# Four edits around the end of the attention stage and the quantized feed-forward: norms in halves, an early gelu table, clamping on ScalarE, and a bias added later

## The chip, the core and the metric

The kernel runs on one core of a Trainium2 chip. A core has engines that run their own instruction streams side by side and meet only at semaphores: TensorE (PE, matrix products; its weight loads are shown as PEld), VectorE (DVE, elementwise work and reductions), ScalarE (ACT, activation functions and copies), GpSimd (POOL, elementwise work) and SyncE (SP, which only issues transfers here). Each engine issues its own stream in order. PE writes its products into a small memory of its own, PSUM; everything else lies in the on-chip memory SBUF. The metric is the device time of one execution in microseconds. Before the change it is 938.37 us, the median of five runs from 937.44 to 939.41.

## What is computed

The input `x` is 32 sequences of 128 tokens of 128 numbers, and so is a context. The reference adds four layers to `x`, each behind a layer norm and a tanh gate:

```python
x = x + jnp.tanh(g_xattn[0]) * _L0_xattn_ref(_layernorm(x, axis=-1), ctx_1024, ctx_1024, ...)
x = x + jnp.tanh(g_ffn[0]) * _L0_ffn_ref(_layernorm(x, axis=-1), ...)
x = x + jnp.tanh(g_xattn[1]) * _L1_xattn_ref(ctx_1024, _layernorm(x, axis=-1))
x = x + jnp.tanh(g_ffn[1]) * _L1_ffn_ref(_layernorm(x, axis=-1), ...)
```

The first layer is an attention of eight heads whose scores are multiplied by decays (an exponential of gates), with a norm of each head's output. The second is a feed-forward with both inputs quantized to 8 bits over the whole tensor:

```python
scale = jnp.maximum((amax - amin) / 255.0, 1e-08)
zp = jnp.clip(jnp.round(-amin / scale) + QMIN, QMIN, QMAX)
q = jnp.clip(jnp.round(x / scale) + zp, QMIN, QMAX)
```

so no token can be quantized before the least and the greatest number of all 32 normed sequences are known; then product with W1, exact gelu, the same quantization again over all hidden values, product with W2, and `+ b`. The third layer aligns the sequences by dynamic time warping, the fourth is a mixture of eight experts with a global threshold. The change touches the end of the first layer and the second.

## The kernel before

Tokens lie on the 128 partitions, one sequence beside the other: `X` is [128, 32, 128]. `YT` holds the normed `X` transposed. A scheduler orders each engine's instructions from the traced program: the earlier traced goes first among those that it takes to be ready, and what is ready may pass what waits. `tc.issue_after(i)` around an instruction puts it behind `i` on the same engine, with no other wait. Tile pools give each tag a fixed number of buffers (`bufs`).

**The attention loop** runs over n = 0 to 32. Round n makes the scores of sequence n+1 on PE (`scores`, L469), and for each half hf of the heads `values(n, hf)`: DVE multiplies scores by decays (`sm`, L505), PE multiplies with the values (L507); then `decays(n+1, hf)`: two products into `bi` (L484, L485) and ACT's exponential `dm` (L490). Every second round ACT copies the product (`ats`, L514), PE transposes it (L523), ACT copies and squares (L527, L529) and DVE takes the denominators (`mxd`, `d2`, L531 to L538): `outputs`.

Every eight sequences a generator `finish(q, ...)` does what is left for them, in steps that the loop takes two at a time behind each half (`for _ in range(2): next(behind, None)`): ACT squares `d2` (L543); DVE makes `qv` (L545) and a reciprocal root in ten small instructions on 64 columns (`root_steps`, L167 to L174), multiplies the heads by it and by the gain and adds to `X` (L557, L562, L567, twice each on 512 columns); then `norm_steps`: bn_stats for each sequence (L140), five small instructions (L145 to L153) and a second root on 8 columns, then for each sequence `y` (L189, four buffers) and its transpose on PE (L192), and for each four sequences `take`: ACT copies into `YT` (L446), DVE reduces greatest and least (`xst`, L448, L449). Sequences 0 to 7, 8 to 15 and 16 to 23 are done so while the next eight are in the loop; the last eight, 24 to 31, all after it.

**The feed-forward's scale.** DVE reduces `xst` (L620); `max_everywhere` (L205 to L213) spreads the two numbers over the partitions by two small PE products; `affine_scale` (L219 to L231) makes the scale, its reciprocal `inv`, the zero point and the bounds `lo` and `hi` in one-column DVE instructions. In the same place DVE makes `b2g` = gate x b2 (L628), and POOL adds it to all of `X` in four instructions (L630).

**The first product.** For each of four groups n of eight sequences and each half k, ACT scales and rounds 512 columns of `YT` (Identity with a large bias, L656), DVE clamps them (L657) and subtracts the bias into the 8-bit integers held as bf16, `XQ` (L659). For each of four chunks c PE multiplies (L664), ACT takes gelu (L669, 1024 columns) and DVE reduces greatest and least into `hst` (L673, L674). ACT also flips and squares context rows (`context_part`, L647 to L651) for the third layer. Then `hs2`, `max_everywhere` and `affine_scale` follow for the hidden values, and `dense` quantizes them with ACT's Relu and one DVE instruction (L708 to L712), the second product (L717) and the addition to `X` (L722).

Of the kernel before, what the change touches and what calls it, by code (L numbers as in the profile page):

```python
# [8 lines left out]
F32 = mybir.dt.float32  # L9
# [9 lines left out]
P = 128  # L19
# [19 lines left out]
def tile_flamingo_gated(  # L39
# [95 lines left out]

    def row_norm_steps(p, v, n, mean, r):

        bn = new(p, [P, n, 6], F32, "bn")
        for i in range(n):
            nc.vector.bn_stats(bn[:, i, :], v[:, i, :])  # L140
            if i % 2 == 1:
                yield

        df = new(p, [P, n], F32, "bn_df")
        nc.vector.tensor_tensor(df, bn[:, :, 1], bn[:, :, 4], ALU.subtract)  # L145
        ve = new(p, [P, n], F32, "bn_ve")
        nc.vector.scalar_tensor_tensor(
            ve, bn[:, :, 2], D * 1e-5, bn[:, :, 5], ALU.add, ALU.add
        )
        nc.vector.scalar_tensor_tensor(mean, df, -0.5, bn[:, :, 1], ALU.mult, ALU.add)  # L150
        yield
        nc.vector.scalar_tensor_tensor(df, df, 0.25, df, ALU.mult, ALU.mult)
        nc.vector.scalar_tensor_tensor(ve, ve, 1.0 / D, df, ALU.mult, ALU.add)  # L153
        yield
        for _ in root_steps(p, ve, n, r):
            yield

    def row_norms(p, v, n):
        mean = new(p, [P, n], F32, "bn_mean")
        r = new(p, [P, n], F32, "bn_r")  # L160
        for _ in row_norm_steps(p, v, n, mean, r):
            pass
        return mean, r

    def root_steps(p, v, n, r):

        nc.vector.tensor_scalar(  # L167
            r.bitcast(I32), v.bitcast(I32), -0.5, 1597463007.0, ALU.mult, ALU.add
        )
        t = new(p, [P, n], F32, "root_t")  # L170
        for _ in range(3):
            nc.vector.tensor_mul(t, r, r)
            nc.vector.scalar_tensor_tensor(t, v, -0.5, t, ALU.mult, ALU.mult)  # L173
            nc.vector.scalar_tensor_tensor(r, t, 1.5, r, ALU.add, ALU.mult)  # L174
            yield

    def norm_steps(p, psp, q, take, tag):

        xq = X[:, 8 * q : 8 * q + 8, :]
        mean = new(p, [P, 8], F32, "bn_mean")  # L180
        r = new(p, [P, 8], F32, "bn_r")
        for _ in row_norm_steps(p, xq, 8, mean, r):
            yield
        for h in range(2):
            tp = new(psp, [P, GB, S], F32, tag)
            for i in range(GB):
                j = GB * h + i
                y = new(p, [P, D], F32, "y", bufs=4)
                nc.vector.tensor_scalar(  # L189
                    y, xq[:, j, :], mean[:, j : j + 1], r[:, j : j + 1], ALU.subtract, ALU.mult  # L190
                )
                nc.tensor.transpose(tp[:, i, :], y, ident)  # L192
                if i % 2 == 1:
                    yield
            take(2 * q + h, tp)
            yield

    def norm_eight(p, psp, q, take, tag="tp"):
        for _ in norm_steps(p, psp, q, take, tag):
            pass  # L200
# [60 lines left out]
    with ExitStack() as st:  # L261
# [218 lines left out]
        def decays(n, hf):  # L480
            r, j, i = n // 16, n % 16 // 4, n % 4
            jr = slice(HW * j, HW * j + HW)
            bi = new(p_bi, [P, 4, S], F32, "bi")
            nc.tensor.matmul(bi, lhsT=identb, rhs=mneg, start=True, stop=False)  # L484
            nc.tensor.matmul(  # L485
                bi, lhsT=GP[jr, r, S * i : S * i + S], rhs=RH[r][jr, 4 * hf : 4 * hf + 4, i, :],
                start=False, stop=True,
            )
            dm = new(hp, [P, 4, S], F32, "dm", bufs=3)
            nc.scalar.activation(dm, bi, AF.Exp)  # L490
            held["dm", n, hf] = dm

        def values(n, hf):
# [11 lines left out]
            nc.vector.tensor_tensor(sm, held["sc", n][:, hf], held.pop(("dm", n, hf)), ALU.mult)  # L505
# [34 lines left out]
        def finish(q, HN, d2, ms):  # L540


            nc.scalar.activation(d2, d2, AF.Square, bias=small_c, scale=1e-3)  # L543
            qv = new(hp, [P, 64], F32, "qv")
# [5 lines left out]
            rr = new(hp, [P, 64], F32, "rr")  # L550
            for _ in root_steps(hp, qv, 64, rr):
                yield
            hf = HN.rearrange("p a x e -> p (a x) e")
            hg = HN.rearrange("p a (s h) e -> p (a s) (h e)", h=NH)
            for k in range(2):
                v = slice(32 * k, 32 * k + 32)
                nc.vector.tensor_tensor(  # L557
                    hf[:, v], hf[:, v], rr[:, v].unsqueeze(2).to_broadcast([P, 32, DH]), ALU.mult
                )
                yield  # L560
                v = slice(4 * k, 4 * k + 4)
                nc.vector.tensor_tensor(  # L562
                    hg[:, v], hg[:, v], gain.unsqueeze(1).to_broadcast([P, 4, D]), ALU.mult
                )
                yield
                xv = X[:, 8 * q + 4 * k : 8 * q + 4 * k + 4, :]
                nc.vector.tensor_tensor(xv, xv, hg[:, v], ALU.add)  # L567
                yield
            for _ in norm_steps(lp, p_at, q, take, "at"):
                yield  # L570
# [9 lines left out]
        for n in range(B + 1):  # L580
            if n < B:
# [6 lines left out]
                for hf in range(2):  # L588
# [5 lines left out]
                    for _ in range(2):  # L594
                        next(behind, None)
            else:
                outputs(n - 1, *tgt)
            if n % 8 == 0 and n:
                for _ in behind:
                    pass  # L600
                behind = finish(n // 8 - 1, *tgt)
# [14 lines left out]
    with ExitStack() as st:  # L616
        fp = pool(st, "ffn")
        HT = new(fp, [P, NC, B * S], F32, "HT")
        xs2 = new(fp, [P, 2], F32, "xs2")
        nc.vector.tensor_reduce(xs2, xst, AX.X, ALU.max)  # L620
        with ExitStack() as st2:
# [5 lines left out]
            b2g = new(fp, [P, D], F32, "b2g")  # L627
            nc.vector.tensor_scalar(b2g, b2s, tgf[:, 0:1], None, ALU.mult)  # L628
            for q in range(4):
                nc.gpsimd.tensor_add(  # L630
                    X[:, 8 * q : 8 * q + 8, :],
                    X[:, 8 * q : 8 * q + 8, :],
                    b2g.unsqueeze(1).to_broadcast([P, 8, D]),
                )
        hst = new(fp, [P, 2, 4 * NC], F32, "hst")
        with ExitStack() as st2:
# [16 lines left out]
            for n in range(4):  # L653
                for k in range(2):
                    blk = YT[:, 8 * n + 4 * k : 8 * n + 4 * k + 4, :].rearrange("p b s -> p (b s)")
                    nc.scalar.activation(blk, blk, AF.Identity, bias=magic_c, scale=inv)  # L656
                    nc.vector.tensor_scalar(blk, blk, lo, hi, ALU.max, ALU.min)  # L657
                    o = 1024 * n + 512 * k
                    nc.vector.tensor_scalar(XQ[:, o : o + 512], blk, MAGIC, None, ALU.subtract)  # L659
                for c in range(NC):  # L660
# [13 lines left out]
                    nc.vector.tensor_reduce(hst[:, 1, o : o + 1], hb, AX.X, ALU.min, negate=True)  # L674
                    if c % 2 == 1:
                        context_part(2 * n + c // 2)
        hs2 = new(fp, [P, 2], F32, "hs2")
# [15 lines left out]
        nc.vector.tensor_mul(s2, s2, tgf[:, 0:1])  # L693
        low = new(fp, [P, 2], F32, "low")
        nc.vector.tensor_scalar(low[:, 1:2], lo, -1.0, None, ALU.mult)
        tie = nc.vector.tensor_scalar(low[:, 0:1], lo, MAGIC, None, ALU.subtract)
# [56 lines left out]
        for n in range(NG):  # L753
# [3 lines left out]
            if n % 2 == 1:  # L757
                for _ in behind:
                    pass
                behind = norm_steps(lp, dps, n // 2, take, "tp")  # L760
# [325 lines left out]
```

## Time and profile before

| what | us |
|---|---|
| median of five runs | 938.37 |
| the profiled execution, and its span | 937.44, 935.7 |
| PE busy in the span | 689.4 (74%) |
| DVE busy | 579.4 (62%) |
| ACT busy | 370.5 (40%) |
| POOL busy | 28.5 (3%) |
| last reduction of the last norms ends | 212.01 |
| first gelu starts | 224.27 |
| last reduction of the gelu's results ends | 264.90 |

The stages follow each other in the span: attention until about 196 us, the last eight norms until 212, the scale of the tokens until 224, the first product until 265, the second product and the distances until 334, the warping until about 440, and the experts, more than half of the span, to the end. Times in the trace count from the span's start. A row of the timeline gives the start, the length, the engine, the line, the operation, the tile written and the tiles read with their shapes (partitions x elements), the number of instructions merged, and in brackets how long the engine had idled and for what. A row of stretches gives the bounds, the length and the busy time of each engine in it, then the granted PE clock (1 is full speed), the DMA's share and its GB/s.

### The profile page before, as it was taken

To read this page: it belongs to the slowest core of one execution; us is meant where nothing else is said; L and a number is where in the kernel's file an instruction comes from. 1 tells how busy PE (TensorE), PEld (TensorE's weight loads), DVE (VectorE), ACT (ScalarE), POOL (GpSimd) and SP (SyncE) were. 2 spreads that over 40 slices of the span, in tenths; PEclk is the share of its full clock that TensorE was granted. 3 is DMA by queue.
4 is the path that set the end of the run, shared out by engine and by line. 5 is a ranking of instruction groups with operands and counts; after the bars stand their busy time and mean duration, and the time that the engine had idled before them with its cause. 6 is when DMAs were issued, how large, how long until landed. Compare 5 with 4: busy or idle time off the path is not lost.

```text
span 935.7 us, 11340 instructions
## 1 busy us (share of the span) xinstructions
PE 689.4 (74%) x4026; PEld 445.1 (48%) x4026; DVE 579.4 (62%) x2011; ACT 370.5 (40%) x624; POOL 28.5 (3%) x66
## 2 busy tenths in 40 slices
PE   0769999933226700000799999999999999999998
PEld 0323333311025400000577767777777777777776
DVE  6665688989988769978666355799232223223232
ACT  1346666547635510000243444434334334334332
POOL 6000000003000000000000000000000000000000
PEclk9968899965556865555699999999999999999999
DMA  9000000031001244420000000000000000000000
GB/s 312 10 11 10 2 2 1 1 127 54 0 0 23 46 106 111 96 59 0 1 1 1 1 1 1 1 12 23 1 1 12 1 12 1 1 12 1 13 1 12
DMA packets 11409, 25.25 MB, mean 27 GB/s; under 512 B 2048, under 2 KB 6688, under 8 KB 10560
## 3 DMA queue, kind: packets, MB, share of 16 engines
q1 hardware_dynamic: 8872, 17.44, 6.2%
q10 hardware_dynamic: 2016, 6.30, 2.7%
q0 software_dynamic: 464, 0.79, 0.3%
q8 instruction: 31, 0.51, 0.2%
q14 instruction: 26, 0.21, 0.1%
HBM read 14.02 MB, written 4.46 MB: 20 GB/s over the span
## 4 chain that ended last, share of the span: by engine, by line
PE 59%; DVE 30%; ACT 4%; DMA 3%; issue 3%; ACTq 0%; DVEq 0%; POOLq 0%
PE mpo L1016 23%; PE mph L1007 20%; DVE ru L837 3%; DVE hit L883 2%; PE sc L469 2%; DVE hst L673 2%; DVE hst L674 2%; DVE ru L836 2%; DVE sm L505 2%; DMA CD<-in_ctx_d 2%; PE at L507 1%; DVE bn L140 1%; PE at L192 1%; PE d L731 1%; DVE root_t L173 1%
## 5 line engine op out<-in xcount | busy, mean ns | idle before, releaser
L1016 PEld LDWEIGHTS mpo<-mw2s,hT 128*128 128x128 f32 x2048 | 252.2, 192 | 62.6 <-issue 39.2
L1010 ACT ACTIVATE hT<-mph,mb1s 128x512 f32<-128x512 f32 x256 | 175.9, 687 | 238.0 <-PE mph L1007 236.3
L1016 PE MATMUL mpo<-mw2s,hT 128*128 128x128 f32 x2048 | 256.4, 276 | 0.1
L1007 PE MATMUL mph<-YT,mw1s 128*128 128x512 f32 x512 | 243.4, 598 | 0.0
L995 DVE SCALAR_TENSOR_TENSOR X<-mpo,GA,X 128x128 f32<-128x128 f32 x192 | 54.0, 343 | 198.1 <-PE mpo L1016 198.1
L1007 PEld LDWEIGHTS mph<-YT,mw1s 128*128 128x128 f32 x512 | 87.6, 192 | 61.9 <-issue 61.8
L995 DVE SCALAR_TENSOR_TENSOR X<-mb2s,GA,X 128x128 f32<-128x128 f32 x256 | 73.0, 342 | 0.0
L790 PE MATMUL gt_ps<-ident,ru 32*128 32x32 f32 x1 | 0.3, 282 | 77.5 <-DVE ru L837 77.5
L505 DVE TENSOR_TENSOR sm<-sc,dm 128x512 f32<-128x512 f32 x64 | 43.5, 684 | 21.8 <-ACT dm L490 18.3
L490 ACT ACTIVATE dm<-bi 128x512 f32<-128x512 f32 x64 | 37.9, 596 | 31.1 <-PE bi L485 28.5
L484 PE MATMUL bi<-mneg,identb 128*128 128x512 bf16 x64 | 26.4, 415 | 24.1 <-DVE identb L112 22.1
L469 PE MATMUL sc<-qm,CD 64*128 64x512 f32 x128 | 43.6, 693 | 0.0
L790 PEld LDWEIGHTS gt_ps<-ident,ru 32*128 32x128 f32 x1 | 0.2, 178 | 77.6 <-issue 77.6
L140 DVE BATCH_NORM_STATS2 bn<-X 128x6 f32<-128x128 f32 x128 | 33.2, 307 | 0.0
L873 ACT COPY dv<-vv 128x8 bf16<-128x8 bf16 (+1 forms) x5 | 1.1, 219 | 77.8 <-DMA rblk<-ru 48.0
L664 PE MATMUL ph<-XQ,w1q 128*128 128x512 bf16 x32 | 14.2, 533 | 23.6 <-DVE XQ L659 18.2
L192 PE MATMUL at<-ident,y 128*128 128x128 f32 x64 | 17.1, 383 | 18.7 <-DVE y L189 16.8
L507 PE MATMUL at<-sm,va 128*32 128x128 f32 x512 | 29.7, 297 | 1.0 <-DVE sm L505 0.8
L837 DVE TENSOR_TENSOR_SCAN ru<-ru,dc 64x128 f32<-64x128 f32 x64 | 26.6, 416 | 4.9 <-DMA dc<-d_dram 2.9
L189 DVE TENSOR_SCALAR y<-X,bn_mean,bn_r 128x128 f32<-128x128 f32 x96 | 27.2, 341 | 1.8 <-PE at L192 1.3
L485 PE MATMUL bi<-RH,GP 32*128 32x512 bf16 x64 | 26.0, 409 | 0.0
L507 PEld LDWEIGHTS at<-sm,va 128*32 128x32 f32 x512 | 11.3, 111 | 29.7 <-issue 7.3
(290 smaller groups left out, 811.2 us busy)
## 6 DMA issues: line engine op xcount, KB each, us to landing
X<-in_x SPq DMA_DIRECT2D x4, 512.0 KB, 11.8
CD<-in_ctx_d ACTq DMA_DIRECT2D x4, 512.0 KB, 10.7
CT<-in_ctx_t SPq DMA_DIRECT2D x4, 512.0 KB, 13.6
mw1s<-in_mw SPq DMA_DIRECT2D x1, 2048.0 KB, 7.6
mw2s<-in_mw SPq DMA_DIRECT2D x1, 2048.0 KB, 12.1
out_x<-X SPq DMA_DIRECT2D x8, 256.0 KB, 2.0
d_dram<-dist SPq DMA_DIRECT2D x15, 128.0 KB, 2.4
rblk<-ru ACTq DMA_DIRECT2D x6, 297.0 KB, 4.4
```

What stands on the lines that cost most here:

```text
L140: nc.vector.bn_stats(bn[:, i, :], v[:, i, :])
L189: nc.vector.tensor_scalar(y, xq[:, j, :], mean[:, j : j + 1], r[:, j : j + 1], ALU.subtract, ALU.mult)
L192: nc.tensor.transpose(tp[:, i, :], y, ident)
L469: nc.tensor.matmul(scs[:, k], lhsT=CD[kr, n, :], rhs=qm[kr, :, n % GB, :], start=True, stop=True)
L490: nc.scalar.activation(dm, bi, AF.Exp)
L505: nc.vector.tensor_tensor(sm, held["sc", n][:, hf], held.pop(("dm", n, hf)), ALU.mult)
L507: last = nc.tensor.matmul(at[HW * c : HW * c + HW, 2 * (n % 2) + hf, :], lhsT=va[:, n % 8 * NH + 4 * hf + c, :], rhs=sm[:, c, :], start=Tr ...
L837: nc.vector.tensor_tensor_scan(ru[:, r + 1, 0, 1 : S + 1], u, dc[:, r, :], BIG, ALU.min, ALU.add)
L995: nc.vector.scalar_tensor_tensor(X[:, b, :], v, gate, X[:, b, :], ALU.mult, ALU.add)
L1007: nc.tensor.matmul(ph, lhsT=mw1s[:, e, c * P : (c + 1) * P], rhs=tok, start=True, stop=True)
L1010: nc.scalar.activation(hT[:, c, :], ph, AF.Gelu_apprx_tanh, bias=mb1s[:, e, c : c + 1])
L1016: nc.tensor.matmul(po[:, i, :], lhsT=hT[:, c, i * S : (i + 1) * S], rhs=mw2s[:, e, c, :], start=(c == 0), stop=(c == NC - 1),)
```

## The change

1. **Norms in two parts.** `finish` and `norm_steps` take a first sequence and a count. Sequences 0 to 23 are done in eights as before; 24 to 27 are begun after round 28, 28 to 31 after round 32. For n over 24 the loop takes three steps behind each half instead of two, and `sm` is put behind the last norm step traced so far that `note` recorded (bn_stats, the ends of the small steps, y, the multiplications and the addition to X; not the reductions).
2. **Gelu table.** After the last exponential ACT runs a gelu on one column, whose result nobody reads.
3. **Clamping on ACT.** A token block is quantized by Identity as before, then Relu with the bias -lo into `XQ`, then one DVE instruction on `XQ` (min with 255, add lo - MAGIC). `lowest` makes the two columns for it; it serves the hidden values too. The blocks of group n+1 are traced behind chunk 0 of group n.
4. **Second bias.** `b2g` and POOL's four additions are traced at the end of group 2, and `b2g` is put behind the last DVE instruction of the last token block.

The hidden values' `s2` and `low` are traced in another order. Tile shapes in the norms are widened to eight and cut, with no effect on what the instructions do.

```diff
     def row_norm_steps(p, v, n, mean, r):
-        bn = new(p, [P, n, 6], F32, "bn")
+        bn = new(p, [P, 8, 6], F32, "bn")[:, 0:n]
         for i in range(n):
-            nc.vector.bn_stats(bn[:, i, :], v[:, i, :])
+            note(nc.vector.bn_stats(bn[:, i, :], v[:, i, :]))
...
-    def norm_steps(p, psp, q, take, tag):
-        xq = X[:, 8 * q : 8 * q + 8, :]
+    def norm_steps(p, psp, s0, n, take, tag):
+        xq = X[:, s0 : s0 + n, :]
...
-        for h in range(2):
+        for h in range(n // GB):
...
-            nc.scalar.activation(dm, bi, AF.Exp)
+            done = nc.scalar.activation(dm, bi, AF.Exp)
             held["dm", n, hf] = dm
+            if n == B - 1 and hf == 1:
+                idle = new(hp, [P, 1], F32, "idle")
+                with tc.issue_after(getattr(done, "ins", done)):
+                    nc.scalar.activation(idle, one_c, AF.Gelu)
...
-            nc.vector.tensor_tensor(sm, held["sc", n][:, hf], held.pop(("dm", n, hf)), ALU.mult)
+            with tc.issue_after(mark["ins"]) if n > 24 else ExitStack():
+                nc.vector.tensor_tensor(sm, held["sc", n][:, hf], held.pop(("dm", n, hf)), ALU.mult)
...
-        def finish(q, HN, d2, ms):
+        def finish(s0, n, HN, d2, ms):
+            pr = slice(s0 % 8 // 2, s0 % 8 // 2 + n // 2)
+            HN, d2, ms = HN[:, pr], d2[:, pr], ms[:, pr]
...
-            for _ in root_steps(hp, qv, 64, rr):
+            for _ in root_steps(hp, qv, 8 * n, rr):
...
-                    for _ in range(2):
+                    for _ in range(3 if n > 24 else 2):
                         next(behind, None)
...
-            if n % 8 == 0 and n:
+            if n in (8, 16, 24, 28, 32):
                 for _ in behind:
                     pass
-                behind = finish(n // 8 - 1, *tgt)
+                part = 4 if n > 24 else 8
+                behind = finish(n - part, part, *tgt)
...
+        def lowest(lo, tag):
+            low = new(fp, [P, 2], F32, tag)
+            nc.vector.tensor_scalar(low[:, 1:2], lo, -1.0, None, ALU.mult)
+            nc.vector.tensor_scalar(low[:, 0:1], lo, MAGIC, None, ALU.subtract)
+            return low
...
-            b2g = new(fp, [P, D], F32, "b2g")
-            nc.vector.tensor_scalar(b2g, b2s, tgf[:, 0:1], None, ALU.mult)
-            for q in range(4):
-                nc.gpsimd.tensor_add(
-                    X[:, 8 * q : 8 * q + 8, :],
-                    X[:, 8 * q : 8 * q + 8, :],
-                    b2g.unsqueeze(1).to_broadcast([P, 8, D]),
-                )
+            low_x = lowest(lo, "low_x")
...
-            for n in range(4):
+            def rounded(n):
                 for k in range(2):
                     blk = YT[:, 8 * n + 4 * k : 8 * n + 4 * k + 4, :].rearrange("p b s -> p (b s)")
                     nc.scalar.activation(blk, blk, AF.Identity, bias=magic_c, scale=inv)
-                    nc.vector.tensor_scalar(blk, blk, lo, hi, ALU.max, ALU.min)
-                    o = 1024 * n + 512 * k
-                    nc.vector.tensor_scalar(XQ[:, o : o + 512], blk, MAGIC, None, ALU.subtract)
+                    xq = XQ[:, 1024 * n + 512 * k : 1024 * n + 512 * k + 512]
+                    nc.scalar.activation(xq, blk, AF.Relu, bias=low_x[:, 1:2])
+                    got = nc.vector.tensor_scalar(xq, xq, 255.0, low_x[:, 0:1], ALU.min, ALU.add)
+                return getattr(got, "ins", got)
+            rounded(0)
+            for n in range(4):
...
+                    if c == 0 and n < 3:
+                        got = rounded(n + 1)
                     if c % 2 == 1:
                         context_part(2 * n + c // 2)
+                if n == 2:
+                    b2g = new(fp, [P, D], F32, "b2g")
+                    with tc.issue_after(got):
+                        nc.vector.tensor_scalar(b2g, b2s, tgf[:, 0:1], None, ALU.mult)
+                    for q in range(4):
+                        nc.gpsimd.tensor_add(
+                            X[:, 8 * q : 8 * q + 8, :],
+                            X[:, 8 * q : 8 * q + 8, :],
+                            b2g.unsqueeze(1).to_broadcast([P, 8, D]),
+                        )
...
-        nc.vector.tensor_mul(s2, s2, tgf[:, 0:1])
-        low = new(fp, [P, 2], F32, "low")
-        nc.vector.tensor_scalar(low[:, 1:2], lo, -1.0, None, ALU.mult)
-        tie = nc.vector.tensor_scalar(low[:, 0:1], lo, MAGIC, None, ALU.subtract)
+        low = lowest(lo, "low")
+        tie = nc.vector.tensor_mul(s2, s2, tgf[:, 0:1])
```

## The prediction

> **What bounds the kernel now.** I read the profile in this order: the shares of the ending chain, the engines' busy time by stretch around the changed code, then the timeline of VectorE (DVE), ScalarE (ACT) and GpSimd (POOL) there.
>
> ```profile
> PE 59%; DVE 30%; ACT 4%; DMA 3%; issue 3%; ACTq 0%; DVEq 0%; POOLq 0%
> ```
>
> ```profile
> 169.50:192.60 23.10, 20.96 (x168) 7.88 (x160) 21.80 (x72) 10.86 (x22) 0.00 (x0) 1.00 0.00 1
> 192.60:196.30 3.70, 1.18 (x14) 0.57 (x12) 1.86 (x5) 2.08 (x5) 0.00 (x0) 0.94 0.00 0
> 196.30:202.84 6.54, 0.00 (x0) 0.00 (x0) 6.15 (x18) 0.00 (x0) 0.00 (x0) 0.50 0.00 0
> 202.84:207.25 4.41, 0.00 (x0) 0.00 (x0) 3.94 (x23) 4.32 (x24) 0.00 (x0) 0.50 1.02 364
> 207.25:212.02 4.77, 2.18 (x8) 1.46 (x8) 4.60 (x13) 4.37 (x21) 0.00 (x0) 0.50 0.99 426
> 212.02:225.50 13.48, 3.00 (x7) 1.11 (x8) 11.87 (x25) 8.52 (x21) 9.24 (x4) 0.50 0.11 44
> 225.50:264.91 39.41, 12.77 (x30) 3.60 (x29) 38.70 (x39) 23.94 (x47) 0.00 (x0) 0.59 0.00 0
> ```
>
> The second fence is the stretches: each gives its length, then busy time of PE, weight loads, DVE, ACT, POOL, granted clock and DMA. The reader should see that DVE is full in every one but the 3.7 us after the last product: in the last six sequences of the attention loop (21.8 of 23.1), in the tail of norms (196.3 to 212.0, PE nearly idle), and in the first feed-forward product (38.7 of 39.4). The change touches only these; what follows 265 us is left as it is.
>
> ```profile
> 212.35 9.24 POOL L630 TENSOR_TENSOR X<-X,b2g 128x1024 f32<-128x1024 f32 x4 [119.10 <-ACT csq L651]
> ...
> 213.12 1.60 DVE L209 TENSOR_SCALAR mmx_dg<-ident,mmx_red 2x2 f32<-2x2 f32 x1
> ...
> 215.59 1.43 DVE L219 TENSOR_TENSOR qx_sc<-mmx 128x1 f32<-128x1 f32 x1
> ...
> 217.31 2.00 DVE L626 TENSOR_TENSOR s<-qx_sc,wsc 128x1 f32<-128x1 f32 x1
> ...
> 219.47 0.15 DVE L225 TENSOR_SCALAR qx_zp<-qx_zp 128x1 f32<-128x1 f32 x1
> ...
> 220.35 1.53 DVE L657 TENSOR_SCALAR YT<-YT,qx_lo,qx_hi 128x512 f32<-128x512 f32 x1
> ...
> 265.90 0.22 DVE L209 TENSOR_SCALAR mmh_dg<-ident,mmh_red 2x2 f32<-2x2 f32 x1
> ...
> 266.99 0.16 DVE L219 TENSOR_TENSOR qh_sc<-mmh 128x1 f32<-128x1 f32 x1
> ```
>
> Start, duration, engine. The four POOL additions of 2.31 us each end at 214.66, 216.97, 219.28 and 221.59; the four long DVE instructions end 0.03 to 0.06 us after the first three, and 0.29 after the last. The same lines run alone at 265.90 and 266.99 in 0.22 and 0.16 us. So these DVE instructions stood still until the POOL addition that ran was over, while the one-column TENSOR_SCALARs between (L225, 0.15 us) did not.
>
> **The change, part by part.**
>
> *A. The last eight norms in two parts of four.* For eight sequences the finishing chain is 11 small instructions on 64 columns (196.31 to 199.14: 0.257 us each), six of 0.605 us, eight bn_stats of 0.195, 15 small ones on 8 columns (204.40 to 207.25: 2.85 us), eight y of 0.267, four reductions of 0.6. Wide work splits without loss. The small ones are paid twice: on 32 columns, between 0.257 and the 8-column pitch of 0.19, 0.225 each, so 22 x 0.225 - 2.83 = +2.1 us, and +2.8 for the second 15. That is +4.9 us of DVE. It is on the path both ways: the first four now run in the last three loop rounds, where DVE has no room (21.8 of 23.1), and only the second four stay behind the loop. The tail after the last product shrinks by about 4.1 us (15.7 to 11.6), but the loop grows by more.
>
> Waits: sm (L505) of sequences 25 to 31 may now issue only behind the last norm step traced. Behind sm on DVE stand only later norm steps; its products on PE, then the next bias product and exponential wait for it, which with 5 us of DVE per round and PE at 3.9 (23.1/6 at the most) has room. The first forced sm no longer fills the 0.3 us while ACT squares d: +0.25. At the end four y instead of eight cover transposes and copy: the reduction waited 0.16 behind eight, and with 1.07 less y it waits 1.2: +1.07. One y pair fills 0.5 of the 3.7 us gap at 192.6, and some of the 0.6 us y wait may go: -0.8 together. A = 4.9 + 0.25 + 1.07 - 0.8 = **+5.4**. Low end: DVE's five kinds of waits in 169.5 to 212 sum to 2.9 us; all gone leaves +2.0. High end: six forced y pairs each waiting the 0.6 of the one seen, 3.6 us more: +9.
>
> *B. The bias additions leave the quantization's scale, and ACT clamps.* From the last reduction's end (212.01) to the first gelu (224.27) are 12.26 us. Undisturbed, the same chain on hst gives the new times: from hs at 264.94 the reciprocal ends at +2.59 and the first low ends at +3.77 (with b2g gone from ahead of it, xs starts 0.04 after the reduction). ACT starts its first Identity 0.09 after the reciprocal, +2.72; two at their 0.73 pitch (3.63 us for five) end at +4.17, later than low. The Relu has no row at this size: between the 512-wide copy (0.58, L446) and the 512-wide Identity (0.80, L656), I take 0.70, pitch 0.61. Second Relu ends +5.5, the min/add (L712's 0.66 pitch on 2048 gives 0.17 on 512, L659's 0.33 bounds it above; 0.22) at +5.75, and the gelu follows the second product's start by 0.62 as at 223.65: +6.4. B = 6.4 - 12.26 = **-5.9**. With Relu straight after low: -6.2. If ACT runs five Identities first, as at 217.48, three x 0.73 come ahead: -3.7. [...]
>
> *C. The 16 gelu blocks.* 32 reductions at 1.127 are 36.06 us; the stage takes 39.40, the rest being three blocks' two DVE passes (0.46 + 0.33 each) and 0.7 of waiting at 246.78. After: six blocks with one pass of 0.22, b2g 0.19: 37.6, so -1.8. ACT carries 16 gelus (18.2), six Identities (4.4), six Relus (3.7) and perhaps four of the eight flip/square groups of 1.8 us, since they start behind the last X addition and now have some 4 us less before the scale is known: 33.5 of 37.6, still under DVE. But the next blocks are traced ahead of the second gelu: 2.7 us of ACT there make the second gelu up to 1.1 late for DVE. I take 0.3: C = **-1.5**, ends -2.1 and -0.3.
>
> The four additions (9.24 us) go on POOL behind the last XQ instruction, beside L673/L674 alone, where POOL is empty and queues nothing until 329.9. I cost them at nothing, since the reductions have one input, like the one-column instructions that ran through; they differ in width, and no row here has both. If that fails, each holds a reduction: +9.2. [...]
>
> *The rest at nothing.* The gelu table (1.28 us at 221.13) lay under DVE's clamp; now it lies under the lag between the last exponential and the last sm, where ACT has 10.9 us of work in 23.1; uncovered it costs at most 1.5. The order of s2 and low near 267.5 swaps instructions of 0.15 on one engine. The 4 MB weight loads on SP start with the last X addition (201.83), some 7 us later, over 200 us before use.
>
> **The sum.** 5.4 - 5.9 - 1.5 = -2.0 us. The profiled execution took 937.44 (span 935.7 and 1.74 around it), giving 935.4; the median of the runs, 938.37, gives **936.4**.
>
> **Rivals.**
> 1. *The split pays.* If the loop's DVE waits absorb the extra instructions, A is +2.0: -5.4 in all, 933.0. For it: PE 21.0 and ACT 10.9 leave room. Against it: DVE waits only 1.3 us in the 23.1, and its work is what grows.
> 2. *The forced order starves DVE in the loop* (slower). sm stands behind y, and y behind PE's transposes, which stand behind products of the sm before. A at +9 gives +1.6, 940.0; with the last gap also unfilled (+0.8), 940.8. It decides from A = 7.4 on, six forced pairs waiting 0.33 on average. For it: y L189 already waited 0.6 with sm free to pass. Against: PE has 2.1 us idle.
> 3. *ACT's order delays the gelus*: five Identities first and the second gelu late, B -3.7 and C -0.3: +1.4, 939.8. For it: five did run first. Against: their DVE partner came late then; now low is ready after one and a half.
> 4. *The additions hold the reductions after all*: +7.2, 945.6.
>
> **How the numbers follow.** A difference of 0.2% (1.9 us) is about what a measurement of this kernel can tell from none. Chances: forecast 0.50 (its own range 934.0 to 938.5: faster 0.29, same 0.20, slower 0.01), rival 1 0.16 (faster), rival 2 0.18 (slower 0.13, same 0.05), rival 3 0.11 (slower 0.04, same 0.07), rival 4 0.05 (slower). Faster 0.45, same 0.32, slower 0.23. The range reaches from A at +2.0 with B and C near their low ends (-6.2, -2.1: 932.1) to rival 2 and a late first gelu (940.8 + 0.7): 932 to 941.5.
>
> **What would show it.** Right: the scale chain's DVE lines at 0.15 to 0.22 us; last xst about 5.4 us later; first gelu 6.4 us after it, not 12.3; 37.9 us of reductions. Wrong: xst no later (1), waits of y and sm in the loop above 3 us (2), a gap between the first two pairs of reductions (3), reductions of over 2 us beside POOL (4). Another order of the whole loop, which the scheduler decides, would make all of it wrong.

## The result: 0.3% slower, and the profile after

The changed kernel takes 941.61 us, the median of 31 runs from 937.24 to 945.98, against 938.16 for the kernel before, the median of 55 runs from 936.05 to 942.26. The ratio is 1.0032 with a 95% interval of 1.0023 to 1.0042: slower by 3.0 us (2.2 to 3.9), where 2.0 less was forecast. The profiled execution took 941.15 us (span 939.4), 3.71 more than the profiled one of before.

First the shares of the ending chain after, which are those of before: no engine took over as the bound of the whole span.

```profile
PE 59%; DVE 30%; ACT 4%; DMA 3%; issue 3%; ACTq 0%; DVEq 0%; POOLq 0%
```

The sum can only be read between marks that both kernels have: the instruction that takes a pair's denominators (`mxd`) for the last sequences of the third eight, the same for the last sequences of all, the end of the last reduction of the norms (`xst`), the first reduction of gelu's results (`hst`), their final reduction (`hs`), and the first Relu on hidden values. Between the first two of them lies the loop whose order the change touches, between the second and the third the tail of norms. Stretches, before (bounds and length; then busy time and instructions of PE, weight loads, DVE, ACT and POOL; granted PE clock; DMA share; GB/s):

```profile
167.97:195.31 27.34, 23.67 (x185) 8.92 (x184) 24.26 (x78) 13.43 (x28) 0.00 (x0) 1.00 0.00 1
195.31:212.01 16.70, 2.18 (x8) 1.46 (x8) 15.26 (x56) 9.03 (x45) 0.00 (x0) 0.52 0.55 218
```

The stretches between the same marks after, and behind them the scale of the tokens and the first product:

```profile
170.67:208.58 37.91, 27.89 (x189) 10.44 (x188) 33.62 (x117) 15.98 (x32) 0.00 (x0) 0.85 0.00 1
208.58:221.46 12.88, 1.15 (x4) 0.73 (x4) 10.34 (x43) 7.09 (x36) 0.00 (x0) 0.50 0.54 201
221.46:229.66 8.20, 2.84 (x7) 1.17 (x8) 3.12 (x18) 7.25 (x19) 0.00 (x0) 0.50 0.47 200
229.66:267.59 37.93, 14.53 (x30) 3.77 (x29) 37.90 (x39) 29.93 (x64) 8.73 (x4) 0.50 0.00 0
```

The table puts lengths against lengths. "Before" of the last four rows comes from the same marks in the trace of before: 212.01, 225.50, 264.94 and 270.01.

| part | before | after | difference | forecast |
|---|---|---|---|---|
| start to the first mark | 167.97 | 170.67 | +2.70 | 0 |
| loop, first mark to last denominators | 27.34 | 37.91 | +10.57 | +9.5 |
| tail of norms, to the last xst | 16.70 | 12.88 | -3.82 | -4.1 |
| scale of the tokens, to the first hst | 13.49 | 8.20 | -5.29 | -5.9 |
| first product, to hs | 39.44 | 37.93 | -1.51 | -1.5 |
| scale of the hidden values, to the first Relu | 5.07 | 6.09 | +1.02 | 0 |

Behind the last mark the two profiled executions differ by less than 0.1 us in all. (The forecast of the loop and the tail together is A, +5.4; the +9.5 is A with the tail's 4.1 added back.)

The first row is not the change: up to there every engine has the same instructions in the same order. Of the 2.70 us, 0.6 had come about by 60 us, and 2.1 came between there and 110, most of it where the clock granted to PE was 0.50 from 100 to 105 us in this execution and 0.97 in that of before. Over the 14 traces of all kernels, the unchanged and the changed, this early stretch costs either little (seven traces, at most 0.4 us) or 1.9 to 2.7 us (seven), in whichever kernel. The remaining rows sum to +0.97, and the runs differ by +3.0.

The loop is not the same in every execution of the changed kernel. Three further traces of it and one of a kernel with the same loop (below) give 37.9 us three times in all and 41.75 twice. With A at 6.75 three times and 10.6 twice, its mean is 8.3, and 8.3 - 5.29 - 1.51 + 1.02 = +2.5 us, within the measured interval. But five traces don't tell how often the loop is long, and the loop is not the only part that varies. One of the two executions with a long loop (e10 below) also took 3.8 us longer from the first Relu on hidden values to the last product of the distances, with the same 240 matmuls at a lower clock. The profiled execution after, then e10:

```profile
273.68:332.16 58.48, 40.03 (x240) 29.45 (x240) 46.89 (x174) 33.48 (x38) 0.00 (x0) 0.72 0.13 28
274.28:336.54 62.26, 43.73 (x240) 31.79 (x240) 46.80 (x174) 33.81 (x39) 0.00 (x0) 0.68 0.13 26
```

So the rows sum to +0.97 with the short loop and to some +4.8 with the long one, and the measured +3.0 lies between; in what shares it is made up of these is not shown.

### The profile page after: what moved, and what is told of

It is laid out like the page before. It is cut to its first block, busy times and chain, and to the rows that moved or that the text cites. A ratio compares the mean times of both kernels' runs of the same rounds, so it can differ in the third digit from the quotient of the medians.

```text
span 939.4 us, 11377 instructions
## 1 busy us (share of the span) xinstructions
PE 697.3 (74%) x4026; PEld 446.9 (48%) x4026; DVE 574.6 (61%) x2031; ACT 376.1 (40%) x634; POOL 28.5 (3%) x66
## 4 chain that ended last, share of the span: by engine, by line
PE 59%; DVE 30%; ACT 4%; DMA 3%; issue 3%; ACTq 0%; DVEq 0%; POOLq 0%
PE mpo L1047 23%; PE mph L1038 21%; DVE ru L868 3%; PE sc L474 3%; DVE hit L914 2%; DVE hst L693 2%; DVE hst L694 2%; DVE ru L867 2%; DVE sm L516 2%; PE at L518 2%; DMA CD<-in_ctx_d 1%; DVE bn L145 1%; PE d L762 1%; DMA w1s<-in_w 1%; PE po L748 1%
## 5 line engine op out<-in xcount | busy, mean ns | idle before, releaser
L516 DVE TENSOR_TENSOR sm<-sc,dm 128x512 f32<-128x512 f32 x64 | 43.6, 685 | 23.1 <-ACT dm L495 19.3
L474 PE MATMUL sc<-qm,CD 64*128 64x512 f32 x128 | 46.0, 715 | 0.0
L748 PE MATMUL po<-w2q,hqt 128*128 128x128 bf16 x128 | 13.4, 285 | 17.9 <-DVE hqt L743 17.9
```

Source lines behind the costliest of these rows:

```text
L474: nc.tensor.matmul(scs[:, k], lhsT=CD[kr, n, :], rhs=qm[kr, :, n % GB, :], start=True, stop=True)
```

## Where the loop's time lies

A can be split further with the busy time of DVE in the two stretches above. Over loop and tail DVE is busy 39.52 us before and 43.96 after, so 4.44 more. It is idle 4.52 before and 6.83 after. Part of that idle time are gaps of less than 0.15 us, most of them between small instructions; they grow by 0.9, from 1.56 to 2.47. The forecast's 4.9 of work counted small instructions from start to start, with these gaps; by that measure the work is 5.35. The rest are waits. In the tail they grow from 0.58 to 1.57, by 1.0, close to the forecast's +1.07 (xst waits 1.19 us for ACT's copy there, 0.16 before). In the loop they were to shrink by 0.55 (0.25 - 0.8), and they grow from 2.38 to 2.77, by 0.4. The three together, 5.35, 1.0 and 0.4, are the 6.75 of A. Of DVE's waits in this loop (engine, tile and line; waited for; us in sum, times, longest) the two that grew:

```profile
DVE xst L453 <- ACT YT L451: 1.5, 1, 1.5
DVE qv L558 <- ACT d L556: 1.0, 2, 0.6
```

Before, xst waited 0.8 us in the loop and qv not at all. The credit of 0.8 did come, with mxd waiting 0.6 less and y 0.3 less, and sm waits 0.4 less too; xst and qv took it back. In the second kind of execution the loop's waits grow to 6.19, by 3.8. The loop of such an execution, a second run of the changed kernel (e10 below):

```profile
167.43:209.18 41.75, 34.83 (x189) 12.24 (x188) 33.90 (x117) 16.01 (x32) 0.00 (x0) 0.67 0.00 1
```

The 189 matmuls of the loop are the same; at a mean clock of 0.67 instead of 0.85 they are busy 34.83 us instead of 27.89. Stretches of 4 us show where the two part. After, the profiled execution:

```profile
182.00:186.00 4.00, 2.92 (x23) 0.90 (x23) 3.69 (x19) 1.67 (x3) 0.00 (x0) 1.00 0.00 0
186.00:190.00 4.00, 3.63 (x27) 1.56 (x28) 3.24 (x15) 2.06 (x5) 0.00 (x0) 1.00 0.00 0
...
194.00:198.00 4.00, 1.94 (x14) 0.55 (x13) 3.73 (x13) 1.07 (x2) 0.00 (x0) 0.92 0.00 0
```

The same kernel in e10, whose marks lie 3.2 us earlier:

```profile
178.00:182.00 4.00, 2.91 (x24) 0.88 (x23) 3.73 (x18) 1.67 (x3) 0.00 (x0) 0.95 0.00 0
182.00:186.00 4.00, 4.00 (x18) 1.32 (x16) 3.49 (x14) 1.82 (x5) 0.00 (x0) 0.50 0.00 0
186.00:190.00 4.00, 4.00 (x16) 1.67 (x16) 1.34 (x7) 0.39 (x2) 0.00 (x0) 0.50 0.00 0
```

In both there is a stretch in which PE was busy 2.9 of 4 us beside a block of norm steps on DVE. In the one the clock stayed at 1.00 behind it up to 197 us and was 0.50 from 198 on; in the other it was 0.50 from about 182 on, PE was full for the next 8 us and more, and DVE, which had been the full engine, was busy 1.34 of 4. Then y waits for PE's transposes, and sm stands behind y. DVE's longest waits in the loop of e10:

```profile
DVE xst L453 <- ACT YT L451: 2.6, 2, 1.5
DVE y L194 <- PE at L197: 2.3, 1, 2.3
```

These norm steps, and the y that waited, are still those of the third eight (16 to 23), not of the first part of the split; the block is eight columns wide, and its last four y start late:

```profile
179.55 0.17 DVE L150 TENSOR_TENSOR bn_df<-bn 128x8 f32<-128x8 f32 x1
...
189.22 1.12 DVE L194 TENSOR_SCALAR y<-X,bn_mean,bn_r 128x128 f32<-128x128 f32 x4 [2.31 <-PE at L197]
```

The three steps a half and the forced sm hold for them too, since n is over 24 there. In the first execution the wait of y was 0.3 us, and PE in turn waited for sm behind the norm steps:

```profile
PE at L518 <- DVE sm L516: 7.5, 11, 1.9
...
DVE y L194 <- PE at L197: 0.3, 1, 0.3
```

Before, PE waited for sm once in this loop, 0.5 us.

## The experiments

All kernels below compute the reference's full output; none leaves work out.

**e1, e3 and e4: the split and the order of s2, each undone, and both.** In e1 the norms of the last eight sequences are whole again, with two steps behind each half and sm free:

```diff
-            with tc.issue_after(mark["ins"]) if n > 24 else ExitStack():
-                nc.vector.tensor_tensor(sm, ...)
+            nc.vector.tensor_tensor(sm, ...)
...
-                    for _ in range(3 if n > 24 else 2):
+                    for _ in range(2):
...
-            if n in (8, 16, 24, 28, 32):
+            if n in (8, 16, 24, 32):
...
-                part = 4 if n > 24 else 8
+                part = 8
```

e3 is the changed kernel with the old order of the hidden values' columns:

```diff
-        low = lowest(lo, "low")
-        tie = nc.vector.tensor_mul(s2, s2, tgf[:, 0:1])
+        nc.vector.tensor_mul(s2, s2, tgf[:, 0:1])
+        low = new(fp, [P, 2], F32, "low")
+        nc.vector.tensor_scalar(low[:, 1:2], lo, -1.0, None, ALU.mult)
+        tie = nc.vector.tensor_scalar(low[:, 0:1], lo, MAGIC, None, ALU.subtract)
```

e4 has both edits.

> The changed kernel with the last eight norms in one part again, the old two steps a half and no order forced on sm; the clamp on ACT, the late bias, the gelu table and the order of the hidden scale stay changed. If the split is what cost (theory): in the two traces the last norm reduction came 6.75 us later relative to the loop's round 24, so this kernel is the kernel before plus -5.3 (scale) -1.5 (first product) +1.0 (hidden scale): about -5.8 us, 932.4. If the loss lies in the PE clock or elsewhere and the split cost only what DVE work it added less its waits (rival, +2.0): the kernel is about 1 us faster than before or no different.

> The changed kernel with s2 and the two columns low traced in the old order, so that the first two instructions on the hidden values (L739) stand behind low again. Theory: in the changed kernel they ran between the zero point's small instructions and put low 2.5 us and the first Relu 1.02 us later after hs; undone, 1.0 us less than the changed kernel, about 2.4 above the kernel before. Rival (that delay is made up in the second product): the same time as the changed kernel, 3.4 above before.

> Both undone: whole norms and the old order of the hidden scale, so only the late bias, the clamp on ACT and the gelu table stay. Theory: -5.3 - 1.5 = -6.8 us against before, 931.4, faster than both kernels. Rival (the parts do not add, because what is won at the scale is lost later to the PE clock or ACT): -3 or less.

Measured against the kernel before (938.41 us on this chip): e1 937.6 us, 0.9986 (0.9973 to 0.9999); e3 939.5, 1.0016 (0.9998 to 1.0033); e4 931.18, 0.9934 (0.9916 to 0.9952). In the traces both parts stand alone. With whole norms the loop takes 28.06 us and the tail 16.70 in both e1 and e4, so A is +0.7 in place of 6.75 to 10.6; the 0.7 is the early gelu's (e8 below). The old order of the columns puts the scale of the hidden values back to 5.07 us within 0.05 in e3 and e4. So the split with its forced order loses, the new order of the columns loses, and without both the change gains 6.2 us by the ratio. e4 beats both kernels. e1, which was expected at 932.4, missed that and came where its rival had it. In its trace the edited parts stand as expected; it is longer by 2.9 us up to the first mark and by 3.5 behind the last. By the medians e1 and e4 are 6.4 us apart, though the order between them is worth 1.0 in the traces; the profiled execution of e1 was 4.8 longer than that of e4, of which 1.0 lies there and 3.2 in the distances stage, where the granted clock was 0.50 from 276 to 290 us and 0.66 from 300 to 320 in e1, and 0.66, 0.81 and 0.84 in those places in e4. The new order is not needed for that: e6 below has the old one, and between the first Relu and the last product of the distances it takes 61.7 us as e1 does, where e4 takes 58.5; and of the four traces of the changed kernel one is long there (e10) and three are not. Whether it makes the long case more frequent isn't settled.

The order of the columns, seen on DVE's timeline of the changed kernel (start, length, engine, line, operation, tiles):

```profile
270.42 1.28 DVE L739 TENSOR_SCALAR HT<-HT,qh_inv 128x2048 f32<-128x2048 f32 x1
271.62 0.15 DVE L230 TENSOR_SCALAR qh_zp<-qh_zp 128x1 f32<-128x1 f32 x1
271.68 1.28 DVE L739 TENSOR_SCALAR HT<-HT,qh_inv 128x2048 f32<-128x2048 f32 x1
272.87 0.15 DVE L231 TENSOR_SCALAR qh_zp<-qh_zp 128x1 f32<-128x1 f32 x1
...
273.43 0.15 DVE L638 TENSOR_SCALAR low<-qh_lo 128x1 f32<-128x1 f32 x1
```

And of the kernel before:

```profile
268.56 0.15 DVE L695 TENSOR_SCALAR low<-qh_lo 128x1 f32<-128x1 f32 x1
...
268.70 2.47 DVE L708 TENSOR_SCALAR HT<-HT,qh_inv 128x2048 f32<-128x2048 f32 x2
```

Before, the two wide multiplications of the hidden values came behind `low`. After, each slipped in ahead of a small instruction of the zero point, and `low`, which the first Relu needs, came two wide instructions later in the order, 5.84 us behind hs instead of 3.62. `tie` is what the code puts later DVE work behind; it was the second `low` and became `s2`, which is ready much earlier.

**e2, e5 and e9: the split without the rest, and the forced order without the split.** e2 is the kernel before with the split of the norms, the three steps and the forced sm; the feed-forward is that of before and there is no early table. e5 is e2 with sm free. e9 is e2 with the norms whole, so it has the three steps and the forced sm and no added small instructions.

```diff
e5 against e2
-            with tc.issue_after(mark["ins"]) if n > 24 else ExitStack():
-                nc.vector.tensor_tensor(sm, ...)
+            nc.vector.tensor_tensor(sm, ...)
e9 against e2
-            if n in (8, 16, 24, 28, 32):
+            if n in (8, 16, 24, 32):
...
-                part = 4 if n > 24 else 8
+                part = 8
```

> The kernel before with the split of the last eight norms alone (three steps a half, sm behind the last norm step), everything behind it as before. Theory: DVE is full in these rounds, so +4.9 us of small instructions and about 1.9 of new waits: +6.8 us, 945. Rival (the waits absorb the work): +2.0, 940. If the forecast's size was right and the trace only caught an unlucky execution: +5.4.

> The split of the last eight norms alone, three steps a half, but sm free to pass the norm steps as before. Theory: the 4.9 us of DVE work stay, and the waits that the forced order made go (sm fills DVE's waits, PE is fed and its granted clock stays at 1.0 until the last round), so the loop and the tail together cost +5 to +6 us, 943.5 to 944.5, with less scatter than the split alone (946.2). Rival (the scheduler now puts the first four norms behind the loop, so nothing is hidden): +6 to +9, no better than the forced order.

> The kernel before with the new order alone: three steps a half and sm behind the last norm step for n over 24, but the last eight norms in one part. It does no more work than the kernel before. If the order costs by itself (theory: PE and sm wait for the norm steps), round 24 to the last denominators takes +1 to +3 us more, and the split's DVE work is the other +5; if the order is free (rival), the loop takes 0 to 0.7 more, as in the three traces with whole norms, and all of the +6.7 to +10.6 is the split's.

Measured: e2 946.18 us, 1.0086 (1.0059 to 1.0113); e5 947.88, 1.0097 (1.0071 to 1.0122); e9 942.76, 1.0046 (1.0033 to 1.0059). The loop of e9:

```profile
169.55:200.60 31.05, 25.77 (x185) 9.65 (x184) 24.52 (x79) 13.73 (x28) 0.00 (x0) 0.95 0.00 1
```

DVE does 24.52 us of work there, 0.26 more than before, and the stretch is 3.71 longer, more than the +1 to +3 expected: the order by itself, three steps and forced sm together, costs some 3.5 us of DVE standing still, at a clock of 0.95. Its longest waits:

```profile
DVE mxd L537 <- ACT sq L535: 2.4, 2, 1.6
DVE sm L511 <- PE sc L474: 1.4, 1, 1.4
DVE y L194 <- PE at L197: 1.3, 1, 1.3
```

Before, the loop's waits were 2.4 us in sum (xst 0.8, mxd 0.6, y 0.6, sm 0.4); these three alone are 5.1. So the price of the order is shown without the split; how it divides between the third step and the forced sm is not, since no run has one without the other on whole norms. e2, which adds the split's work, is slower again: +11.76 in the loop, -3.83 in the tail, and -1.40 in the scale of the tokens, since in e2 and e5 `b2g` is made in the gap ahead of the last xst and POOL's first addition runs beside these reductions. The two prices don't add, though: the waits in the loop are 3.7 us in e2, 5.8 in e9. Freeing sm (e5) doesn't mend it: its traced loop is 2.0 us shorter than e2's, with waits of 3.0, more than the 2.8 of the changed kernel's short loop with sm forced, and by the median e5 is no faster, 947.88 where the theory had at most 944.5. Its traced execution, 940.71 us, was the fastest of six, the others being 947.5 to 950.3; the mean granted clock was 0.864 in the one and 0.848 to 0.852 in the others. What they did in the loop has no trace.

**e6: products added in the loop.** The expectation takes the falling clock for an effect of PE's waits for sm. That was the author's estimate, and no run shows it by itself. e6 adds work for PE: it is e2 with the score products of rounds 25 and up computed twice into the same place:

```diff
-                for k in range(2):
+                for k in (0, 1, 0, 1) if n > 24 else (0, 1):
```

> The split alone with the forced order, and the score products of rounds 26 to 31 made twice (the second overwrites the first with the same numbers): 1.1 us more of PE work in each of six rounds. If PE's granted clock fell in these rounds because PE waited for sm (theory), it now stays at 1.0 until the last round, and loop plus tail cost less than the +7.9 of the split alone's trace, +5.5 to +6.8, although PE does 7 us more. Rival (the waits are those of DVE's order and the clock has no part): the same +8 or more, since work was only added.

Measured: 952.65 us, 1.0150 (1.0136 to 1.0165). Its loop:

```profile
171.70:211.08 39.38, 32.26 (x213) 12.32 (x212) 33.61 (x118) 14.76 (x30) 0.00 (x0) 0.92 0.00 1
```

The mean clock is 0.92, against 0.67 to 0.85 in the five traces with the changed kernel's loop, and the loop is still 12.04 longer than before. So a higher clock, with this work added, doesn't bring the time back; PE is busy 32.26 us in the loop. The run rules out that the clock alone carries the loss, not that it carries a part.

**e7: the bias moved, alone.** The kernel before, with `b2g` and the four POOL additions traced at the end of the last group and put behind the last token block:

```diff
-            b2g = new(fp, [P, D], F32, "b2g")
-            nc.vector.tensor_scalar(b2g, b2s, tgf[:, 0:1], None, ALU.mult)
-            for q in range(4):
-                nc.gpsimd.tensor_add(...)
...
+                if n == 3:
+                    b2g = new(fp, [P, D], F32, "b2g")
+                    with tc.issue_after(getattr(got, "ins", got)):
+                        nc.vector.tensor_scalar(b2g, b2s, tgf[:, 0:1], None, ALU.mult)
+                    for q in range(4):
+                        nc.gpsimd.tensor_add(...)
```

> The kernel before with b2g and the four POOL additions moved behind the last token block, nothing else. If POOL's additions held the DVE instructions (theory), the scale chain shrinks from 12.26 to about 6.8 us between the last norm reduction and the first gelu, and the first product is unchanged: -5.4 us in all, 933.0, so that the clamp on ACT brings nothing at the scale and only the -1.5 in the first product. Rival (the clamp on ACT is what shortened it): -1 or less. Rival (the additions now hold the reductions): +1 to +4.

Measured: 934.68 us, 0.9960 (0.9947 to 0.9972), so -3.75 us by the ratio and -4.4 between the marks of the trace, where -5.4 was expected; the first product is unchanged. DVE's timeline of e7 in the scale of the tokens:

```profile
213.78 0.22 DVE L209 TENSOR_SCALAR mmx_dg<-ident,mmx_red 2x2 f32<-2x2 f32 x1
...
214.86 0.16 DVE L219 TENSOR_TENSOR qx_sc<-mmx 128x1 f32<-128x1 f32 x1
...
215.32 0.14 DVE L626 TENSOR_TENSOR s<-qx_sc,wsc 128x1 f32<-128x1 f32 x1
...
216.57 0.55 DVE L649 TENSOR_SCALAR YT<-YT,qx_lo,qx_hi 128x512 f32<-128x512 f32 x1
```

The four instructions that took 1.60, 1.43, 2.00 and 1.53 us beside POOL take 0.22, 0.16, 0.14 and 0.55. That DVE stood still for POOL, and that it was worth most of B, is shown by this one edit. None of the four reads what POOL writes, so in the kernel before DVE and POOL meet at more than semaphores.

**e8: e4 without the early gelu table.**

```diff
-            if n == B - 1 and hf == 1:
-                idle = new(hp, [P, 1], F32, "idle")
-                with tc.issue_after(getattr(done, "ins", done)):
-                    nc.scalar.activation(idle, one_c, AF.Gelu)
```

> The fastest so far (whole norms, old order of the hidden scale, clamp on ACT, late bias: 931.2) without the early gelu. The table of 1.28 us is then loaded ahead of the first gelu. Theory: ACT waits there for PE anyway, less than the load is long, so the first gelu comes 0 to 0.8 us later: 931.2 to 932.0. Rival (the load was under other work before and is so now): no difference; or, if the two extra Identities ahead of the first gelu stay where they are, the full +1.3.

Measured: 936.08 us, 0.9981 (0.9968 to 0.9994), against e4's 0.9934, so outside all that was expected. In the traces the scale of the tokens is 1.4 us longer than in e4. ACT's timeline of e8:

```profile
219.73 1.28 ACT L683 ACT_TABLE_LOAD   x1
221.02 1.20 ACT L683 ACTIVATE HT<-ph,b1s,s 128x1024 f32<-128x1024 f32 x1
```

And of e4, where the load came early:

```profile
220.54 1.50 ACT L671 ACTIVATE YT<-YT,magic_c,qx_inv 128x512 f32<-128x512 f32 x2
221.95 1.19 ACT L688 ACTIVATE HT<-ph,b1s,s 128x1024 f32<-128x1024 f32 x1
```

The load of 1.28 us ends 0.01 us before the first gelu in e8, and in e4 the gelu follows the Identities at once. So early loading is worth 1.4 us at this place. It has a price in the loop, where the load (1.28 us at 193.01 in e4) stands ahead of ACT's last copies. The loops of e4, with it, and of e8, without:

```profile
170.24:198.30 28.06, 23.51 (x185) 8.94 (x184) 24.19 (x79) 14.71 (x30) 0.00 (x0) 0.97 0.00 1
168.63:195.97 27.34, 23.66 (x185) 8.91 (x184) 24.26 (x79) 13.43 (x28) 0.00 (x0) 1.00 0.00 1
```

e8's loop is as long as that of the kernel before, and e4's 0.7 longer, with xst waiting 1.4 us for ACT instead of 0.8; so the early load is worth 0.7 us in all between these two traces. The two ratios to the kernel before lie further apart, by 0.0047 or 4.4 us; the mean granted clocks of the two kernels' executions differ too (0.856 and 0.861), and the rest isn't explained.

**e10, e11 and e12: the changed kernel again**, unedited, one execution each, to see how often the loop takes which length.

> The changed kernel itself, another profiled execution. Theory: scale -5.3, first product -1.5, hidden scale +1.0, each within 0.1 of the other trace, and loop plus tail +6.7 to +10.6, the larger where PE's granted clock falls to 0.5 early in the last rounds. Rival: the other parts scatter too, and loop plus tail stays at +6.7.

> The changed kernel once more: the same as for the other copy. With the traces so far loop plus tail would average about +8.4 and the whole change +2.6, near the measured +3.2.

> A third copy of the changed kernel: the same. If loop plus tail is +6.7 in all three, the measured +3.2 is not explained by the parts, and the rest lies in the PE clock ahead of the change (the 1.8 us at round 2 to 7).

Measured: 945.66, 941.22 and 939.95 us, with loops of 41.75, 37.91 and 37.92. e3, which has the same loop, had 41.75. The tail, the scale of the tokens and the first product agree within 0.02 us in all of them. Against the first profiled execution, e10's 4.5 us are 3.8 in the loop and 3.9 behind the last mark, less 3.2 up to the first. The mean clock in the loop was 0.67 in the two long ones and 0.82 to 0.85 in the three short ones.

## Why the prediction was wrong

The sign was wrong, and 941.61 lies just outside the range of 932 to 941.5. By its own steps:

- **A, the norms in two parts: the step that failed.** Forecast +5.4, measured +6.75 or +10.6, on the mean of five traces 8.3. The work was nearly right: 5.35 against 4.9 from start to start, with small instructions on 32 columns at 0.225 us as interpolated. The tail's extra wait was right: 1.0 against 1.07. What failed is the step that the forced sm has room, with PE at 3.9 us a round, and that the loop's waits therefore fall by 0.55 on balance. They rose by 0.4 us in three traces and by 3.8 in two. In the three, the credit of 0.8 came, but xst and qv waited longer by 0.6 and 1.0, of which the forecast had 0.25. In the two, y waited 2.3 us instead of 0.6 and xst 2.6 instead of 0.8, while PE's mean clock in the loop was 0.67. e9 shows that the order can cost this much without the split: with the norm steps ahead of sm the waits on mxd, sm and y bring DVE's idle time up by some 3.5 us, with next to no work added. How much of the split kernel's loss is the forced sm's stays open, since e5 frees it and is no faster. Room on an engine as a mean over a round says nothing of when its inputs come.
- **Rival 2, the forced order, was near, but its sign did not show.** A passed its point of decision, 7.4, on the mean of the traces. But y and sm together, which were to wait above 3 us in the loop, waited 0.3 in the short loops and 2.3 in the long ones; in the short ones, three of five, this is less than the 0.9 of the kernel before. Only in the long ones did a long wait come at the place it named (sm behind y, y behind PE's transposes), and xst's rise of 1.8 us there was as large as y's 1.7. What it left out is the granted clock: in two of five traces its mean in the loop was 0.67, and in that of e10 it was 0.50 from the norms of the third eight on. Its "against", PE's 2.1 us of idle time in 23.1, was taken at a clock of 1.00, though the stretches shown from 196.3 to 225.5 us stood at 0.50, and a loop with norm steps in it could have been costed at both.
- **B, the scale of the tokens**: forecast -5.9, measured -5.29. The DVE lines are at 0.14 to 0.22 us as forecast, and the first Relu came right behind two Identities. But the first gelu started 6.96 us after the last xst, not 6.4, because two more Identities ran ahead of it:

```profile
226.38 0.71 ACT L674 ACTIVATE XQ<-YT,low_x 128x512 bf16<-128x512 f32 x1
227.00 1.50 ACT L672 ACTIVATE YT<-YT,magic_c,qx_inv 128x512 f32<-128x512 f32 x2
228.42 1.20 ACT L689 ACTIVATE HT<-ph,b1s,s 128x1024 f32<-128x1024 f32 x1
```

  That is the milder part of rival 3; the 0.71 us of the Relu is the forecast's 0.70.
- **C, the first product**: forecast -1.5, measured -1.51, with 37.93 us against "37.9 us of reductions".
- **The POOL additions at nothing: right.** They ran at the end of the same stretch. POOL's timeline, and DVE's beside it:

```profile
258.86 9.26 POOL L705 TENSOR_TENSOR X<-X,b2g 128x1024 f32<-128x1024 f32 x4 [164.68 <-ACT csq L667]
```

```profile
259.60 1.21 DVE L694 TENSOR_REDUCE hst<-HT 128x1 f32<-128x1024 f32 x1
260.72 1.20 DVE L693 TENSOR_REDUCE hst<-HT 128x1 f32<-128x1024 f32 x1
```

  The reductions keep their length of 1.21 us and their pitch of 1.12 beside POOL, so rival 4 is out. The row that was missing before now stands. It was near for the next step: the last addition ended at 268.12, and the hidden scale's 2x2 instruction, of the kind that took 1.60 us beside POOL before, started at 268.56 and took 0.22.
- **The gelu table at nothing: not shown for this kernel.** At the scale the early load saves 1.4 us (e8), since the cover it had before, DVE's clamp, goes with this same change; the forecast's B had no load in its chain, so that is in its sum. In the loop it was said to lie under a lag; with whole norms it cost 0.7 us there (e4 against e8). What it costs with split norms no run shows.
- **The order of s2 and low at nothing: wrong by 1.02 us.** It was said to swap instructions of 0.15 us on one engine. In fact it changes which DVE work may pass `low`, and two instructions of 1.28 us passed.

Summed: A, from 5.4 to 8.3, adds 2.9, B 0.6, C 0, the columns 1.0. Together 4.5, from the forecast of -2.0 to +2.5, near the measured +3.0; the 8.3 rests on five traces. With the short loop alone A adds 1.35, and the sum is +0.97: the sign is wrong even then.

## What to carry to other kernels

An order forced to fill one engine has to be costed by when each producer delivers, not by mean room on it: on whole norms the order alone cost 3.5 us with next to no work added, half of the 6.8 that the same change won in the two stretches behind it. POOL's additions did no harm beside DVE's reductions, which kept their pitch of 1.12 us; moving them there, with nothing else, won 3.75 us. When an instruction that others are ordered behind is replaced, look at what may now pass it.

## What was not expected of the hardware

Executions of the changed kernel differ by up to 8.7 us, and the time follows the mean granted clock of PE: it falls by 0.53 us for each 0.001 of mean clock (correlation -0.95), while the kernel before has a slope of 0.21 and a correlation of -0.37. The mean is over the whole span, so the early place and the distances, whose lengths vary too, are in it. In the five traces with whole norms and sm free (before, e1, e4, e7, e8) the mean clock in the loop was 0.97 to 1.00; with the split and the forced order PE drops to 2.9 of 4 us busy in the middle of it, and the mean was 0.67 in two of the five traces with this loop and 0.82 to 0.85 in three. Behind such a stretch the clock was 1.00 from 186 to 197 us in the profiled execution, and in e10 it was 0.50 from 182 to 190, where PE was busy all the 8 us. So that the clock fell is shown, and why it fell in some executions only is not.

Also open: what the slower executions of e5 did in the loop; and why e4 and e1, and e4 and e8, lie 6.4 and 4.4 us apart in their times where their traces part by 1.0 and 0.7 in the edited places.
